# Counting the first 64 neighbours: triangular matmuls on TensorE against running sums along rows on VectorE

## The chip, the cores and the metric

The kernel runs on one core of a Trainium2 chip. The metric is the device time of one execution in microseconds (us). Five engines of the core work beside each other, each through its own queue in order: TensorE (PE in the profile), VectorE (DVE), ScalarE (ACT), GpSimd (POOL) and SyncE (SP, which here only issues transfers). They wait for each other by semaphores.

## The reference, cut to what matters

Four graph layers work on the same x (2708 x 512) and the same adjacency matrix adj (2708 x 2708, integers). Each layer's result is added to its input and normalised. The change concerns layer 0 and how its masks reach layer 1:

```python
# layer 0
Ab = A > 0
keep = Ab & (jnp.cumsum(Ab.astype(jnp.int32), axis=1) <= 64)      # the first 64 neighbours of each row
cnt = keep.sum(axis=1, keepdims=True)
nb_mean = (keep @ X) / jnp.maximum(cnt, 1.0)
xj = leaky_relu(nb_mean @ W_nb.T + b_nb)
xi = leaky_relu(X @ W_line.T + b_line)
x = layernorm(X + xi + jnp.where(cnt > 0, xj, 0))
# layer 1
mask = adj > 0                                                     # all neighbours
agg = mask @ x / jnp.maximum(mask.sum(axis=1, keepdims=True), 1.0)
x = layernorm(x + relu(concat(x @ W_self + b_self, agg @ W_nb + b_nb) @ W_comb + b_comb))
```

Layers 2 and 3 are attention over the same mask, and a small network at the end.

## The kernel before, in words

The 2708 rows are cut into NT = 22 tiles of 128 (the last has 20). Layers 0 and 1 run in four stages, which this text calls L0a, L0b, L1a and L1b.

**L0a, one t per row tile (lines 283 to 304).** Each t computes two products of x with a weight: P0 = x W_nb' into the single buffer pm0, and P1 = x W_line' into the single buffer pm1 (`product`, line 229: four matmuls of fp32, 512 columns wide, each in two passes). ScalarE and VectorE split P0 into a high and a low half, yH and yL, that stay in SBUF (lines 223, 224; yL frees pm0). P1 gets its bias and leaky ReLU on VectorE (298, 190; the add frees pm1), the row tile of x is added on GpSimd (300), and the sum goes to r0_dram (301). Beside this the adjacency matrix is brought in: `load_mask` (242) loads 128 rows of adj as bf16 through GpSimd's queue, `count` (248) makes them 0 or 1 on VectorE and sums each row, four small operations keep the row's counts (250 to 253), and `turn` (262, 266) transposes the row tile on PE, 22 transposes, and copies it as fp8 into maskT, from where every later layer reads it. maskT has one plane per tile j of neighbours, and in it one column per row of adj.

**L0b, masked sums (lines 311 to 429).** The row tiles are taken in blocks: first tiles 20 and 21, then five blocks of four. For each block and each of the 22 planes j, `kept` makes the operand kT: two matmuls of the 0/1 plane with constant triangles (line 319 with `upper`, line 409 with `below`) keep a running count in PSUM, and one VectorE operation (321) compares it with 64 and multiplies by the mask. kT has two buffers. Then, per row tile of the block, two matmuls add kT times yH and kT times yL (416): eight for a block of four. At the block's end ScalarE scales the sums by the reciprocal count (426). What follows (`finish`, lines 329 to 338) is a generator: one step of it is taken at each j of the next block. It adds the bias, applies leaky ReLU, adds r0, normalises and stores x1. Two more generators, `weights1` (products of layer 1's weights, on PE) and `vectors` (sums of weights for the later layers, on VectorE), are taken in steps beside it.

**L1a (lines 432 to 444)** makes two products per row tile of x1, with the same buffers pm0 and pm1. **L1b (445 to 464)** multiplies the whole mask with them: ScalarE casts planes of maskT to fp32r (455), PE takes 968 matmuls (458).

**The order of the work.** The program's order and priorities give each engine a fixed queue when the kernel is built. In L0a, `pe` chains some PE instructions by hand in program order. `issue_after` puts operations behind a named instruction of the program. [...] an engine whose next instruction waits lets everything behind it wait.

Of the kernel before, what the change touches and what calls it, by code (L numbers as in the profile page):

```python
# [9 lines left out]
F32 = mybir.dt.float32  # L10
F32R = mybir.dt.float32r
BF16 = mybir.dt.bfloat16
F8 = mybir.dt.float8e4
AF = mybir.ActivationFunctionType
OP = mybir.AluOpType
# [3 lines left out]
P = 128  # L19
D = 512  # L20
KD = D // P
EPS = 1e-5
ALPHA = 0.2
KEEP = 64.0
# [6 lines left out]
def kernel(  # L31
# [9 lines left out]
    nc = tc.nc  # L41
# [8 lines left out]
    def rows(t):  # L50
        return min(P, N - t * P)
# [24 lines left out]
    for c, value in ((iso, 0.0), (has, 0.0), (rdeg, 1.0), (rkeep, 1.0)):  # L76
        nc.vector.memset(c, value)
# [4 lines left out]

    maskT = big.tile([P, NT, NT * P], F8, name="maskT")
    nc.gpsimd.memset(maskT[:, NT - 1, :], 0.0)
    nc.gpsimd.memset(maskT[:, :, N:], 0.0)
# [47 lines left out]
    def transpose_weight(pool, psum, dst, src):  # L133

        for ki in range(KD):
            wr = pool.tile([P, D], F32, name="wr", bufs=4)
            nc.sync.dma_start(wr, src[ki * P:(ki + 1) * P, :])
            ps = psum.tile([P, KD, P], F32, name="ps_tr")
            for ko in range(KD):
                pe(nc.tensor.transpose(ps[:, ko, :], wr[:, ko * P:(ko + 1) * P], ident))  # L140
            nc.vector.tensor_copy(dst[:, :, ki * P:(ki + 1) * P], ps)  # L141
# [47 lines left out]
    def leaky(dst, u):  # L189
        nc.vector.scalar_tensor_tensor(dst, u, 0.01, u, op0=OP.mult, op1=OP.max)  # L190
# [7 lines left out]
    with ExitStack() as phase:  # L198
        yp = phase.enter_context(tc.tile_pool(name="y", bufs=1))

        upper = yp.tile([P, P], BF16, name="upper")
        make_upper_triangular(nc, upper)
        below = yp.tile([P, P], BF16, name="below")
        nc.vector.tensor_scalar(below, upper, -1.0, 1.0, op0=OP.mult, op1=OP.add)
# [16 lines left out]

        def keep_y(t, n, pm):
            nc.scalar.copy(yH[:n, t, :], pm[:n])  # L223
            return nc.vector.tensor_sub(yL[:n, t, :], pm[:n], yH[:n, t, :].bitcast(F32))
# [6 lines left out]

        def rows_of(src):
            return early(2, NT, lambda t: fetched(src, t, rows(t)))

        with ExitStack() as ph:
            st = ph.enter_context(tc.tile_pool(name="l0a", bufs=2))
            wnT, wlT = weight(), weight2

            def load_mask(t):
                n = rows(t)  # L240
                m = st.tile([P, N], BF16, name="m")
                nc.gpsimd.dma_start(m[:n], adj[t * P:t * P + n, :], max_dma_last_dim=N * 2)
                return m

            def count(t, m):
                n = rows(t)
                cnt = sm.tile([P, 1], F32, name="cnt")
                nc.vector.tensor_scalar(m[:n], m[:n], 0.0, None, op0=OP.is_gt, op1=OP.add, accum_out=cnt[:n])
                one = slice(t, t + 1)
                nc.vector.tensor_scalar(iso[:n, one], cnt[:n], 0.0, None, op0=OP.is_equal)  # L250
                nc.vector.tensor_scalar(has[:n, one], cnt[:n], 0.0, None, op0=OP.is_gt)
                nc.vector.tensor_scalar(rkeep[:n, one], cnt[:n], KEEP, 1.0, op0=OP.min, op1=OP.max)
                nc.vector.tensor_scalar(rdeg[:n, one], cnt[:n], 1.0, None, op0=OP.max)

            def turn(t, m, order=as_it_comes):
                n = rows(t)
                for g0 in range(0, NT, G):
                    g1 = min(g0 + G, NT)
                    ps = sums(BF16, (P, G, P))
                    for j in range(g0, g1):  # L260
                        w = rows(j)
                        order(nc.tensor.transpose(ps[:w, j - g0, :n], m[:n, j * P:j * P + w], identb[:n, :n]))
                    parts = [(P, g0, min(g1, FULL))] + ([(rows(FULL), FULL, NT)] if g1 > FULL else [])
                    for w, a, b in parts:
                        if a < b:
                            nc.scalar.copy(maskT[:w, a:b, t * P:t * P + n], ps[:w, a - g0:b - g0, :n],
                                           saturate=False)

            xs = rows_of(x)
            xTs = early(0, NT, lambda t, order=as_it_comes: transposed(ahead, ps_tr, xs(t), rows(t), "xT", order))
            ms = {}

            transpose_weight(st, ps_tr, wnT, l0_w_nb)
            lows = {}
            for t in range(2):
                xT = xTs(t, order=pe)
                lows[t] = keep_y(t, P, product(xT, P, wnT, 0, pe))
            transpose_weight(st, ps_tr, wlT, l0_w_line)  # L280
            b_line = bias(bcast(l0_b_line, D))
            for i in range(2):
                ms[i] = load_mask(i)
            for t in range(NT):
                n = rows(t)
                order = pe if t < 3 else as_it_comes
                if t > 1:
                    lows[t] = keep_y(t, n, product(xTs(t), n, wnT, 0, order))
                xT = xTs(t)
                if t + 1 < NT:  # L290
                    xTs(t + 1)
                for q in range(0 if t == 2 else t - 1, t) if t > 1 else ():
                    turn(q, ms[q], order)
                    if q + 2 < NT:
                        ms[q + 2] = load_mask(q + 2)
                pm = product(xT, n, wlT, 1, order)
                u = sm.tile([P, D], F32, name="u")
                nc.vector.tensor_add(u[:n], pm[:n], b_line[:n])
                leaky(u[:n], u[:n])
                nc.gpsimd.tensor_add(u[:n], u[:n], xs(t))  # L300
                nc.gpsimd.dma_start(r0_dram[t * P:t * P + n, :], u[:n])
                with tc.issue_after(lows[t].ins):
                    count(t, ms[t])
            turn(NT - 1, ms[NT - 1])
            nc.vector.reciprocal(rkeep, rkeep)
            nc.vector.reciprocal(rdeg, rdeg)

# [3 lines left out]
        with ExitStack() as ph:  # L311
            st = ph.enter_context(tc.tile_pool(name="l0b", bufs=1))
            b_nb = bias(bcast(l0_b_nb, D))
            cuts = [(b, min(b + 4, NT)) for b in range(0, NT, 4)]
            cuts = cuts[-1:] + cuts[:-1]

            def kept(cum, b, j):
                cols, w = slice(b[0] * P, b[1] * P), (b[1] - b[0]) * P
                nc.tensor.matmul(cum[:, :w], upper, maskT[:, j, cols], start=(j == 0), stop=True, skip_group_check=True)  # L319
                kT = st.tile([P, 512], F32R, name="kT", bufs=2)  # L320
                nc.vector.scalar_tensor_tensor(kT[:, :w], cum[:, :w], KEEP, maskT[:, j, cols],  # L321
                                               op0=OP.is_le, op1=OP.mult)
                return kT

            def begin(b):
                cum = ps_mm.tile([P, D], F32, name="pm0")
                return cum, kept(cum, b, 0)

            def finish(ts_, us):
                for t in ts_:  # L330
                    n, u = rows(t), us[t]
                    r0 = fetched(r0_dram, t, n)
                    nc.vector.tensor_add(u[:n], u[:n], b_nb[:n])
                    leaky(u[:n], u[:n])
                    yield
                    nc.vector.scalar_tensor_tensor(u[:n], u[:n], has[:n, t:t + 1], r0, op0=OP.mult, op1=OP.add)
                    layer_norm(sm, u[:n], n, u[:n])
                    nc.gpsimd.dma_start(x1_dram[t * P:t * P + n, :], u[:n])
                    yield
# [61 lines left out]
            todo, later = iter(()), chain(weights1(), vectors())  # L401
            cum, kT = begin(cuts[0])
            for i, b in enumerate(cuts):
                ts_ = range(*b)
                cols, w = slice(b[0] * P, b[1] * P), (b[1] - b[0]) * P
                pa = {t: sums() for t in ts_}
                for j in range(NT):
                    if j + 1 < NT:
                        nc.tensor.matmul(cum[:, :w], below, maskT[:, j, cols], start=False, stop=True,
                                         skip_group_check=True)  # L410
                        nxt = kept(cum, b, j + 1)
                    elif i + 1 < len(cuts):
                        cum, nxt = begin(cuts[i + 1])
# [5 lines left out]
                    next(todo, None)  # L419
                    if i == 1 and j > 1 or i > 1 and j % 2 or i == 0 and j == 2:  # L420
                        next(later, None)
# [6 lines left out]
            for _ in later:  # L428
                pass
# [4 lines left out]
            for t in range(NT):  # L434
                n = rows(t)
                xT = xTs(t)
                keep_y(t, n, product(xT, n, wnb[0], 0))
                if t + 1 < NT:
                    xTs(t + 1)
# [855 lines left out]
```

## Time and profile before

The three runs took 3095.4, 3096.92 and 3097.85 us. The profiled execution spans 3089.8 us at a mean granted clock of 0.99.

| Engine | busy, us | share of the span |
|---|---|---|
| PE | 2969.2 | 96% |
| VectorE | 1963.5 | 64% |
| ScalarE | 1411.1 | 46% |
| GpSimd | 239.6 | 8% |

| Stage | from, us | to, us |
|---|---|---|
| L0a | 0 | 214.9 |
| L0b | 214.9 | 532 |
| L1a | 532 | 694 |
| L1b | 694 | 921 |
| layers 2 and 3 | 921 | 3089.8 |

How to read it: the page gives busy time by engine, a table of 40 slices of about 77 us each, transfers, the chain that ended last, and groups of instructions. A group's row has the line, the engine, the operation, what it writes and reads with partitions x elements and type, a count, the busy time with the mean of one in ns, and the idle time of the engine just before with what ended it. In rows of waits, the numbers are the total in us, the times, and the longest. Durations of matmuls overlap, so their spacing is read from start times.

### The profile page before, as it was taken

The page shows a single profiled execution, that of the slowest core. Times are in us where ns is not written, and L with a number is a line of the kernel's source. Part 1 is how long each engine was busy: PE and PEld are TensorE (multiplying, and loading weights), DVE is VectorE, ACT ScalarE, POOL GpSimd, SP SyncE. Part 2 cuts the span into 40 slices and gives each one's busy share as a digit, 9 for nine tenths or more (in the row PEclk, how much of TensorE's full clock was granted, in tenths as well). Part 3 has the DMA queues.
Part 4 walks back from the last instruction along what each step waited for, and adds up shares of the span by engine and source line. Part 5 has one row for each costly group of instructions (what it writes and reads, how often), then busy time and mean ns, then how long its engine had stood idle before and what let it go on. Part 6 is the DMA issues. An engine that isn't in the chain of part 4 may idle for free. (4 is left out here: it accounts for less than half of the span.)

```text
span 3089.8 us, 36801 instructions
## 1 busy us (share of the span) xinstructions
PE 2969.2 (96%) x14714; PEld 1644.4 (53%) x14714; DVE 1963.5 (64%) x2495; ACT 1411.1 (46%) x1590; POOL 239.6 (8%) x378
## 2 busy tenths in 40 slices
PE   8999999999999999999998999999969999999997
PEld 4556666448888433444466333443446455555555
DVE  5662765212233899999976999999944535344242
ACT  2431000112225699999965899999942000001001
POOL 2220010101110000000012000000000000100001
PEclk9999999999999999999999999999989999999999
DMA  6651521312222001011034000000052000000000
GB/s 142 142 124 35 121 67 38 109 60 90 73 74 84 15 29 47 28 38 34 22 107 153 29 29 28 28 27 27 18 156 63 4 14 17 31 14 15 14 21 20
DMA packets 112920, 168.93 MB, mean 55 GB/s; under 512 B 39716, under 2 KB 63141, under 8 KB 112738
## 3 DMA queue, kind: packets, MB, share of 16 engines
q1 hardware_dynamic: 84066, 105.02, 11.4%
q0 software_dynamic: 18784, 57.79, 6.5%
q10 hardware_dynamic: 9888, 3.67, 0.5%
q8 instruction: 118, 1.93, 0.2%
q14 instruction: 64, 0.52, 0.1%
HBM read 136.46 MB, written 44.64 MB: 59 GB/s over the span
## 5 line engine op out<-in xcount | busy, mean ns | idle before, releaser
L624 DVE SCALAR_TENSOR_TENSOR e<-v_bc,ucol,maskT 128x1300 f32<-128x1300 f32 (+3 forms) x836 | 1183.2, 1474 | 335.0 <-PE pn L926 318.8
L632 ACT ACTIVATE c<-e,bcol 128x1300 fp8e4<-128x1300 f32 (+1 forms) x704 | 994.6, 1424 | 82.7 <-DVE e L624 32.8
L782 PE MATMUL po<-e,R 128*64 128x512 f32 (+2 forms) x4224 | 924.9, 549 | 29.9 <-DVE e L624 28.2
L782 PEld LDWEIGHTS po<-e,R 128*64 128x64 f32 x4224 | 349.0, 136 | 573.2 <-issue 383.2
L926 PE MATMUL pn<-e,R 128*128 128x512 f32 (+1 forms) x1056 | 415.1, 544 | 0.0
L926 PEld LDWEIGHTS pn<-e,R 128*128 128x128 f32 x1056 | 192.1, 191 | 199.8 <-issue 196.7
L416 PE MATMUL acc<-yH,kT 128*128 128x512 f32 x484 | 214.8, 444 | 0.0
L894 ACT ACTIVATE w<-pl,b 128x256 f32<-128x256 f32 (+1 forms) x88 | 40.9, 465 | 373.3 <-PE pl L892 373.3
L458 PE MATMUL acc<-yL,mf 128*128 128x512 f32 x484 | 192.9, 399 | 0.0
L416 PE MATMUL acc<-yL,kT 128*128 128x512 f32 x484 | 192.3, 397 | 0.0
L458 PE MATMUL acc<-yH,mf 128*128 128x512 f32 x484 | 190.5, 394 | 0.0
L117 POOL TENSOR_TENSOR ln_rs<-ln_rs,half 128x1 f32<-128x1 f32 x88 | 54.5, 620 | 1676.4 <-DVE ln_rs L116 1674.5
L561 PE MATMUL pm<-w,xT 128*128 128x264 f32 (+1 forms) x704 | 168.3, 394 | 10.7 <-DVE R L575 5.2
L229 PE MATMUL pm<-w,xT 128*128 128x512 f32 (+1 forms) x384 | 173.2, 593 | 2.4 <-ACT xT L130 1.4
L229 PE MATMUL pm<-weight,xT 128*128 128x512 f32 (+1 forms) x352 | 162.0, 604 | 3.6 <-DVE weight L141 2.8
L321 DVE SCALAR_TENSOR_TENSOR kT<-pm,maskT 128x512 fp32r<-128x512 f32 (+1 forms) x132 | 84.8, 642 | 123.5 <-PE pm L319 123.0
L892 PE MATMUL pl<-lin 128*128 128x256 f32 (+1 forms) x704 | 154.8, 374 | 2.8 <-DVE lin L811 2.8
L901 PE MATMUL pl<-lin,w 128*128 128x512 f32 (+1 forms) x352 | 157.4, 593 | 0.0
L561 PEld LDWEIGHTS pm<-w,xT 128*128 128x128 f32 (+1 forms) x704 | 129.6, 189 | 38.0 <-issue 5.8
L892 PEld LDWEIGHTS pl<-lin 128*128 128x128 f32 x704 | 130.6, 192 | 33.4 <-issue 15.8
L455 ACT CAST mf<-maskT 128x1024 fp32r<-128x1024 fp8e4 (+1 forms) x66 | 64.4, 977 | 163.4 <-PE acc L458 154.1
L223 ACT CAST yH<-pm 128x512 fp32r<-128x512 f32 (+1 forms) x44 | 25.7, 585 | 243.6 <-PE pm L229 243.6
(186 smaller groups left out, 2619.9 us busy)
## 6 DMA issues: line engine op xcount, KB each, us to landing
rows<-x_dram SPq DMA_DIRECT2D x63, 256.0 KB
m<-in_adj_dram POOLq DMA_DIRECT2D x21, 677.0 KB, 6.2
v_bc<-v_dram SPq DMA_DIRECT2D x16, 704.0 KB
x_dram<-u POOLq DMA_DIRECT2D x42, 256.0 KB, 2.3
v_bc<-v_dram SPq DMA_DIRECT2D x16, 650.0 KB
rows<-in_x_dram SPq DMA_DIRECT2D x21, 256.0 KB
r_dram<-u POOLq DMA_DIRECT2D x21, 256.0 KB, 3.2
rows<-r_dram SPq DMA_DIRECT2D x21, 256.0 KB
```

The source lines that it names most:

```text
L229: order(nc.tensor.matmul(pm[:n], xT[:, k, :n], w[:, k, :], start=(k == 0), stop=(k == KD - 1)))
L321: nc.vector.scalar_tensor_tensor(kT[:, :w], cum[:, :w], KEEP, maskT[:, j, cols], op0=OP.is_le, op1=OP.mult)
L416: nc.tensor.matmul(pa[t], kT[:, (t - b[0]) * P:(t - b[0] + 1) * P], y[:, j, :], start=(j == 0 and y is yH), stop=(j == NT - 1 and y is yL))
L455: nc.scalar.copy(mf[:, :g1 - g0, :], maskT[:, g0:g1, t * P:(t + 1) * P])
L458: nc.tensor.matmul(pa, mf[:, j - g0, :], y[:, j, :], start=(j == 0 and y is yH), stop=(j == NT - 1 and y is yL))
L561: nc.tensor.matmul(pm[a][:n, :D // 2 + heads], xT[:, k, :n], w[:, k, a, :D // 2 + heads], start=(k == 0), stop=(k == KD - 1))
L624: nc.vector.scalar_tensor_tensor(e[:, :w], v[:, :w], ucol[:, j, h:h + 1], maskT[:, j, c0:c0 + w], op0=OP.max, op1=OP.mult)
L632: nc.scalar.activation(c[:, :w], e[:, :w], AF.Sigmoid, bias=bcol[:, j, h:h + 1], scale=STEP, saturate=False)
L782: pe(nc.tensor.matmul(po[i][HO * k:HO * k + HO, :c1 - c0], R2[:, j, h * HO:(h + 1) * HO], e[:, c0:c1], start=(j == 0), stop=(j == NT - 1)))
L892: nc.tensor.matmul(pl[:, :w], self.lin1[:, k, f * P:(f + 1) * P], h[:, k, :w], start=(k == 0), stop=(k == KD - 1))
L901: nc.tensor.matmul(pl[:n], gT[:, f, (t - t0) * P:(t - t0) * P + n], self.lin2[:, f, :], start=(f == 0), stop=(f == KF - 1))
L926: nc.tensor.matmul(pn[k][:, :w], R2[:, j, k * P:(k + 1) * P], e[:, :w], start=(j == 0), stop=(j == NT - 1))
```

## The change

The counting on PE goes. Instead the count runs along the rows before they are turned:

- `count` moves to ScalarE: a sigmoid with a very steep slope makes the row 0 or 1 in place and sums it.
- `place` on VectorE: a scan adds along the row from -64.5 and takes the minimum with 0.5, in bf16; its product with the 0/1 row is negative for a kept neighbour, 0.5 for one that is dropped, 0 elsewhere. It is done in two parts of 1354 elements in L0a, and in four parts of 677 in L0b.
- `turn` copies to maskT with Sign: maskT now holds -1, 1 and 0.
- `kept` is one Relu of -maskT on ScalarE. No counting matmul and no VectorE operation is left in it.
- In L1a, one VectorE operation per plane (not_equal 0) makes maskT 0/1 again for all that follow.
- Fifteen of the 22 row tiles (HERE = 15, in the order of the blocks) are counted and turned in L0a, the first at t = 1 and with one t in six left out; the other seven go through a generator `other_masks`, ahead of `weights1` and `vectors`, one step at each j of L0b, in buffers lent by the weight tile "w" and by "spare". A turn in L0a comes at least a t after its count.
- All of L0a's PE instructions are chained by hand (`pe`).
- x is added in `finish`, from a second load, by VectorE; GpSimd's add goes. `finish` takes a step at every second j.
- The small operations on the counts are done per block (`reciprocals`) or once.
- The weights of layer 0 are staged in planes of maskT; the memsets of maskT come behind the first mask loads.

```diff
-            def count(t, m):
-                nc.vector.tensor_scalar(m[:n], m[:n], 0.0, None, op0=OP.is_gt, op1=OP.add, accum_out=cnt[:n])
...
+        def count(i, m):
+            nc.scalar.activation(m[:n], m[:n], AF.Sigmoid, bias=gate[:n], scale=STEP, accum_out=cnts[:n, t:t + 1])
+        def place(i, m, places, part, of):
...
+            nc.vector.tensor_tensor_scan(places[:n, :c1 - c0], m[:n, c0:c1], over[:n].to_broadcast([n, c1 - c0]),
+                                         places[:n, c0 - N * (part - 1) // of - 1:][:, :1] if part else -KEEP - 0.5,
+                                         OP.add, OP.min)
+            return nc.vector.tensor_mul(m[:n, c0:c1], m[:n, c0:c1], places[:n, :c1 - c0])
...
-                            nc.scalar.copy(maskT[:w, a:b, t * P:t * P + n], ps[:w, a - g0:b - g0, :n],
+                        nc.scalar.activation(maskT[:w, a:b, t * P:t * P + n], ps[:w, a - g0:b - g0, :n], AF.Sign,
...
+                now = counted < min(HERE, -(-t * HERE // (NT - 4)))
+                if now:
+                    m, places = masks(counted), st.tile([P, N // 2], BF16, name="places", bufs=1)
+                    with tc.issue_after(highs[t].ins):
+                        count(counted, m)
+                    with tc.issue_after(lows[t].ins):
+                        place(counted, m, places, 0, 2)
...
-                nc.gpsimd.tensor_add(u[:n], u[:n], xs(t))
...
+                if now:
+                    with tc.issue_after(low.ins):
+                        place(counted, m, places, 1, 2)
...
-            def kept(cum, b, j):
-                nc.tensor.matmul(cum[:, :w], upper, maskT[:, j, cols], start=(j == 0), stop=True, skip_group_check=True)
-                nc.vector.scalar_tensor_tensor(kT[:, :w], cum[:, :w], KEEP, maskT[:, j, cols],
-                                               op0=OP.is_le, op1=OP.mult)
...
+            def kept(b, j):
+                kT = st.tile([P, 4 * P], F32R, name="kT", bufs=2)
+                made = nc.scalar.activation(kT[:, :w], maskT[:, j, b[0] * P:b[0] * P + w], AF.Relu, scale=-1.0)
...
+                    nc.vector.tensor_add(u[:n], u[:n], x0)
...
-                        nc.tensor.matmul(cum[:, :w], below, maskT[:, j, cols], start=False, stop=True,
-                                         skip_group_check=True)
...
-                    next(todo, None)
-                    if i == 1 and j > 1 or i > 1 and j % 2 or i == 0 and j == 2:
-                        next(later, None)
+                    if j % 2:
+                        next(todo, None)
+                    with tc.issue_after(nxt_made.ins):
+                        next(both, None)
...
+                nc.vector.tensor_scalar(maskT[:, t, :], maskT[:, t, :], 0.0, None, op0=OP.not_equal, saturate=False)
```

## The prediction

> **What bounds the kernel now.** I read the slices of the page first: TensorE (PE) stands at 9 almost throughout. Then the busy times by stretch, cut where the stages of layers 0 and 1 begin and end by the times of their lines: L0a (projections, counting, turning of masks) 0 to 214.9 us, L0b (masked sums) to 532, L1a to 694, L1b to 921. The columns are PE, weight loads, VectorE (DVE), ScalarE (ACT), GpSimd (POOL), clock, DMA.
>
> ```profile
> 125.00:214.90 89.90, 89.90 (x443) 46.40 (x442) 54.39 (x99) 35.88 (x61) 24.77 (x29) 1.00 0.60 135
> 482.00:532.00 50.00, 49.56 (x214) 34.93 (x213) 25.50 (x48) 1.16 (x3) 5.14 (x8) 1.00 0.13 43
> 545.00:694.00 149.00, 149.00 (x406) 68.11 (x405) 34.73 (x56) 23.61 (x43) 14.47 (x27) 1.00 0.25 84
> 694.00:921.00 227.00, 227.00 (x975) 183.07 (x974) 64.41 (x128) 62.37 (x64) 24.54 (x44) 1.00 0.23 76
> ```
>
> PE has no idle time in any of them, so each microsecond taken from PE counts, and each wait given to PE counts. The groups by line show what the change removes (L319, L409: counting matmuls; L321, L248: DVE), and the waits show how little PE waits for:
>
> ```profile
> L321 DVE SCALAR_TENSOR_TENSOR kT<-pm,maskT 128x512 fp32r<-128x512 f32 (+1 forms) x132 | 84.8, 642 | 123.5 <-PE pm L319 123.0
> L248 DVE TENSOR_SCALAR_CACHE_REDUCE m<-m 128x2708 bf16<-128x2708 bf16 (+1 forms) x22 | 65.2, 2964 | 9.7 <-DMA m<-in_adj_dram 9.7
> L319 PE MATMUL pm<-maskT,upper 128*128 128x512 fp8e4 (+1 forms) x132 | 47.9, 363 | 0.0
> L409 PE MATMUL pm<-maskT,below 128*128 128x512 fp8e4 (+1 forms) x126 | 46.7, 371 | 3.6 <-DVE kT L321 3.6
> ```
>
> A matmul's duration overlaps its neighbours', so I price them by start times, in order of time on PE:
>
> ```profile
> 481.25 0.39 PE L409 MATMUL pm<-maskT,below 128*128 128x512 fp8e4 x1
> 481.48 0.38 PE L319 MATMUL pm<-maskT,upper 128*128 128x512 fp8e4 x1
> 481.50 0.59 PE L416 MATMUL acc<-yH,kT 128*128 128x512 f32 x1
> ...
> 483.80 0.38 PE L319 MATMUL pm<-maskT,upper 128*128 128x512 fp8e4 x1
> 483.82 0.59 PE L416 MATMUL acc<-yH,kT 128*128 128x512 f32 x1
> ```
>
> One j of a four-tile block takes 483.82 - 481.50 = 2.32 us. In L1b, where no counting runs, 968 matmuls (L458) take 225.8 us, 0.2333 each; eight are 1.87. So counting costs PE 0.45 us per j, and in the two-tile block (1.167 per j against 0.933) 0.23.
>
> [...]
>
> **The change, part by part.** DVE unit prices: from L248 (2708 elements, 2964 ns) and 512 elements at 690, one element costs 1.04 ns and an instruction 0.15 us.
> - Scan of 1354 elements: at half throughput 2 x 1354 x 1.04 + 150 = 2.96 us (bounds 1.56 at full rate, 4.4 at three cycles). Its product in bf16: 0.86 (1.56 at one per cycle). Quarters of 677: 1.57 and 0.51.
> - not_equal over 2816 fp8: 1.62 (bound 3.1).
> - Sigmoid over 2708 on ACT: 1.466 + 1300 x 0.833 ns = 2.55 us. Relu for kT: near 0.6 (the 512-wide copy L130, 585 ns).
>
> *L0b, PE.* Removed: 110 x 0.454 + 22 x 0.234 = **-55 us**. Seven turns arrive from L0a, 22 transposes in 1.42 us each (start times at 130.03 and 131.45): **+9.9**.
>
> *L0b, new waits.* kT moves from DVE to ACT, with two buffers: ACT may be late by at most one j. A Relu starts when j begins; a sigmoid behind it holds the next one. In the two-tile block (0.93 per j, Relu 0.4): 0.5 + 2.55 + 0.5 = 3.6 against two j = 1.9, so PE waits 1.7 us, and 2.2 at the second sigmoid, with a turn's last copies (0.72 and 0.26, the rows of L266) in the queue too; in the other blocks 0.6 + 2.55 + 0.6 = 3.75 against 3.73, with those copies 0.5 to 1.1 for each of five, 3.2 together. PE also waits in its queue at a turn until DVE has done the scans: a mask needs 4 x (1.57 + 0.51) = 8.3 us on DVE after its sigmoid. In the two-tile block PE gets there early: 14.4 us after L0b's begin for the second group of mask 15's transposes, which needs the last quarter, ready at 7.7 + 0.1 + 8.6 = 16.4; 2.0, and likewise 1.0 for mask 16. In the next blocks the built order lets six j (11 us) pass first; only for mask 20, whose scans stand behind 24 us of the previous block's finish (four tiles of nine DVE operations), do I find 3.6 us. Sum: 3.9 + 3.2 + 3.0 + 3.6 = **+14** (bounds 7 and 25). L0b: -55 + 9.9 + 14 = **-31**.
>
> *L0a.* Per t PE has 8.83 us (P0 to P0, 126.16 and 134.99), or 7.4 without a turn: seven turns gone, **-9.9**. On DVE the count (2.96 plus five small ones) goes; a t with a mask now has 3 x 0.69 + 2 x (2.96 + 0.86) = 9.7, about 9.4 since neighbours overlap by some 0.06. Fifteen masks fall on five of each six t. PE needs 5 x 8.83 + 7.4 = 51.6 us for six. DVE: the first mask's scan waits 2.5 for its sigmoid (put behind yH), 5 x 9.4, then P0 of the next t (3.6) waits until yL has freed the single pm0, then 1.5 to the next yL: 54.6. So DVE sets L0a: 3 x 3.0 = **+9**. L0a: **-1** (bounds -10 and +12). Mask loads (6.2 us to landing) land before ACT is ready for them. The added table load (1.28) and the scan ahead of the fourth weight copy lie in the start, where PE already waits 2.8 for that copy; some 1.8 is in the bounds.
>
> *L1a.* The 22 not_equal: in the built order eleven run in L0b's last block, under 41 us of PE, eleven at L1a's beginning. There DVE has, before the first yL, four of them (6.5) and nine finish operations (6.1): yL(0) comes some 16 us after L0b's end in place of 8, and the second product needs pm0. **+7.5**; the later ones add 1.2. Together **+9** (bounds 2 and 25).
>
> *At no cost.* POOL's add of x (27.9 us, L300) goes; its place, 22 DVE adds of 0.69 in finish, lies under L0b's PE, as do 22 more loads of x on SP's queue (DMA share 0.13 to 0.58). Weight rows stage in maskT: same transfers. The memsets of maskT (4.5 us) move behind the first mask loads, where POOL is idle for 24 us. POOL's later mask loads wait for turns, and the layer norm's pow stands behind them: DVE waits for pow, counted in the 3.6. L1b and all later layers read 0/1 masks as before.
>
> Sum against the profiled span: -31 - 1 + 9 = **-23 us**, 3089.8 to 3067. The other runs (3095.4 to 3097.9, median 3096.9) stand 7 us above the span, so I forecast 3074.
>
> **The rivals.**
> - *DVE hides everywhere.* For: DVE is busy only 54 of 90 and 25 of 50 us. Against: its queue is in order and carries the releases of pm0 and pm1. Then -55, and only the sigmoid waits (+7) stay: 3049.
> - *The bf16 product runs one per cycle.* [...] Then 15 x 1.4 = 21 us more in L0a, some 4 in L0b: 3074 + 25 = 3099, no change.
> - *Slower: the scan is dearer than half throughput.* At three cycles 1.4 more for each of 30 halves in L0a, 42 us, and 7 x 4 x 0.7 = 20 in L0b, of which some 15 reach PE: -23 + 57, 3131. It decides from about 0.55 us over 2.96 per half (23 / 42 of the step), 3.5 us. For: no scan is in the trace, and each has a scalar operand and a broadcast input. [...]
> - *PE doesn't get shorter* (the counting was hidden). L1b's 0.2333 per matmul, with the same weight loads, excludes it; I give it nothing.
>
> **How the numbers follow.** Likeliest 0.55, 3074, [...] (own range 3060 to 3086); hidden 0.18, 3049; product 0.13, 3099; scan 0.14, 3131. 3046 to 3098 leaves out the scan case, half of the product case and the fringe below. A measurement tells 0.2% (6 us) from no change: faster 0.55 + 0.18 + 0.01 = 0.74; within 0.11; slower 0.15.
>
> **What would show it.** Right: no L319 or L409; one j in blocks of four at 1.87 us; scans near 2.96 and 1.57 us, products 0.86 and 0.51, not_equal 1.62; L0a ending near 214, L0b taking some 286 us, L1a some 171; PE waits on ACT's kT of one or two microseconds after each sigmoid, and on DVE's yL in L0a and at L1a's start. Wrong: a scan above 3.5 us; PE waits at turns well beyond 10 us in all; L0a beyond 225; or no waits at all.

## The result, and the profile after

The changed kernel takes 3064.78 us (median of 3062.05, 3063.23, 3066.34 and 3068.42) against 3097.39 for the kernel before on the same chip: a ratio of 0.9896, 95% interval 0.9879 to 0.9914, or 32.6 us less. The prediction was 3074.

The busy times by stretch, cut where the four stages begin and end, of the kernel before and then of the changed one (columns: length, then PE, weight loads, DVE, ACT and POOL with their instructions, clock, DMA share, GB/s):

```profile
0.00:214.90 214.90, 202.12 (x957) 107.20 (x958) 124.51 (x216) 78.91 (x131) 60.90 (x76) 0.99 0.62 139
214.90:532.70 317.80, 314.20 (x1327) 215.22 (x1327) 176.89 (x319) 22.08 (x40) 24.69 (x38) 0.99 0.24 66
532.70:694.50 161.80, 161.08 (x440) 73.67 (x438) 42.50 (x71) 26.32 (x48) 16.14 (x30) 1.00 0.26 86
694.50:920.70 226.20, 226.20 (x971) 182.77 (x971) 64.11 (x127) 62.37 (x64) 24.33 (x43) 1.00 0.23 76
```

```profile
0.00:221.40 221.40, 197.63 (x802) 98.91 (x802) 160.78 (x151) 101.19 (x138) 30.01 (x48) 0.98 0.47 110
221.40:503.60 282.20, 270.05 (x1223) 204.06 (x1223) 174.61 (x274) 132.25 (x209) 32.10 (x41) 0.99 0.41 109
503.60:671.80 168.20, 163.12 (x441) 74.34 (x439) 68.58 (x91) 26.44 (x48) 21.55 (x32) 0.98 0.28 90
671.80:891.50 219.70, 219.70 (x971) 181.95 (x971) 64.13 (x127) 62.43 (x64) 24.34 (x43) 1.00 0.24 79
```

| Stage | before, us | after, us | difference | forecast |
|---|---|---|---|---|
| L0a | 214.9 | 221.4 | +6.5 | -1 |
| L0b | 317.8 | 282.2 | -35.6 | -31 |
| L1a | 161.8 | 168.2 | +6.4 | +9 |
| L1b | 226.2 | 219.7 | -6.5 | 0 |
| layers 2 and 3 | 2169.1 | 2173.1 | +4.0 | 0 |
| span | 3089.8 | 3064.6 | -25.2 | -23 |

The spans differ by 25.2 us and the medians by 32.6, because the profiled execution of the kernel before was short for its kind. A copy of that kernel with 32 bytes of padding (the second run below; its time is the same, ratio 1.0007) has a span of 3097.6, of which its layers 2 and 3 take 2174.8. Against that execution the stages differ by +5.8, -37.0, +6.4, -6.5 and -1.7: -33.0 us. So the +4.0 in the later layers is the difference between two executions and not a cost of the change.

The unit prices are in the groups by line and shape (busy time and mean ns of one, then idle time before):

```profile
L253 DVE TENSOR_TENSOR_SCAN places<-m,over 128x1354 bf16<-128x1354 bf16 x14 | 41.6, 2970 | 6.6 <-ACT m L247 6.3
L256 DVE TENSOR_TENSOR m<-m,places 128x1354 bf16<-128x1354 bf16 x28 | 24.1, 862 | 0.7
L253 DVE TENSOR_TENSOR_SCAN w<-w,over 128x677 bf16<-128x677 bf16 x16 | 25.7, 1609 | 24.2 <-ACT w L247 24.0
L484 DVE TENSOR_SCALAR maskT<-maskT 128x2816 fp8e4<-128x2816 fp8e4 x22 | 35.1, 1617 | 0.0
L247 ACT ACTIVATE m<-m,gate 128x2708 bf16<-128x2708 bf16 x14 | 35.7, 2553 | 0.0
L335 ACT ACTIVATE kT<-maskT 128x512 fp32r<-128x512 fp8e4 x110 | 68.8, 630 | 108.8 <-PE acc L459 108.8
```

Scan 2.97 us (3.03 for a row's second half), product 0.86, quarter scan 1.61, not_equal 1.62, sigmoid 2.55, Relu 0.63: all as priced, the quarter scan and the Relu 0.03 to 0.04 dearer.

Three of the prices on VectorE had no line behind them when they were forecast: the trace of the kernel before has no scan, no bf16 product and no not_equal on fp8. The changed kernel shows them. From a part of 677 elements to one of 1354 the scan adds 1.361 us (1609 to 2970 ns), so 2.01 ns per element, about twice the 1.04 ns that the forecast took from L248; the product adds 0.352 us (510 to 862 ns), so 0.52 ns per element, half of it; the not_equal, less 0.15 us for the instruction, comes to 0.52 ns for each of its 2816 elements. The sigmoid's price had lines in the trace before: 1466 ns for 1408 elements on ACT (L632), and 0.833 ns for each element more (L838: 1056 ns for 1024, 696 for 592).

What PE waits for, over layers 0 and 1 (the seven largest rows; total, times, longest):

```profile
PE pm L229 <- DVE yL L224: 9.3, 11, 1.6
PE ps_tr L137 <- POOL maskT L295: 6.2, 1, 6.2
PE pm L265 <- DVE spare L256: 6.0, 4, 2.4
PE pm L229 <- ACT xT L127: 5.8, 2, 5.1
PE pm L229 <- DVE weight L138: 5.2, 1, 5.2
PE acc L459 <- ACT kT L335: 4.3, 6, 1.6
PE pm L265 <- DVE w L256: 1.8, 1, 1.8
```

The 6.2 us are the start, before any weight is there (5.6 before). The rest is what the change made PE wait for: yL in L0a, the turns (6.0 and 1.8) and kT in L0b, and two single waits, of 5.2 us for a weight at the start and of 5.1 us for xT at L1a's begin. What the waits don't show is L1b: no PE wait there in either kernel, and still it takes 6.5 us less.

### The profile page after: what moved, and what is told of

It is laid out like the page before. It is cut to its first block, busy times and chain, and to the rows that moved or that the text cites. A ratio compares the mean times of both kernels' runs of the same rounds, so it can differ in the third digit from the quotient of the medians.

```text
span 3064.6 us, 36494 instructions
## 1 busy us (share of the span) xinstructions
PE 2918.2 (95%) x14456; PEld 1623.1 (53%) x14456; DVE 2021.9 (66%) x2408; ACT 1545.0 (50%) x1768; POOL 220.9 (7%) x354
## 5 line engine op out<-in xcount | busy, mean ns | idle before, releaser
L459 PE MATMUL acc<-yH,kT 128*128 128x512 f32 x484 | 197.3, 408 | 4.3 <-ACT kT L335 4.3
L459 PE MATMUL acc<-yL,kT 128*128 128x512 f32 x484 | 189.8, 392 | 0.0
L505 PE MATMUL acc<-yH,mf 128*128 128x512 f32 x484 | 188.4, 389 | 0.0
L505 PE MATMUL acc<-yL,mf 128*128 128x512 f32 x484 | 188.3, 389 | 0.0
L335 ACT ACTIVATE kT<-maskT 128x512 fp32r<-128x512 fp8e4 (+1 forms) x132 | 77.6, 594 | 118.8 <-PE acc L459 118.7
```

Source lines behind the costliest of these rows:

```text
L335: made = nc.scalar.activation(kT[:, :w], maskT[:, j, b[0] * P:b[0] * P + w], AF.Relu, scale=-1.0)
L459: nc.tensor.matmul(pa[t], kT[:, (t - b[0]) * P:(t - b[0] + 1) * P], y[:, j, :], start=(j == 0 and y is yH), stop=(j == NT - 1 and y is yL))
L505: nc.tensor.matmul(pa, mf[:, j - g0, :], y[:, j, :], start=(j == 0 and y is yH), stop=(j == NT - 1 and y is yL))
```

## The experiments

### Why do unchanged matmuls run faster?

In L1b both kernels run the same 968 matmuls on operands of the same types. The timeline of PE in the kernel before and in the changed one (start, duration):

```profile
799.64 0.39 PE L458 MATMUL acc<-yH,mf 128*128 128x512 f32 x1
799.87 0.40 PE L458 MATMUL acc<-yL,mf 128*128 128x512 f32 x1
800.10 0.39 PE L458 MATMUL acc<-yH,mf 128*128 128x512 f32 x1
800.33 0.40 PE L458 MATMUL acc<-yL,mf 128*128 128x512 f32 x1
```

```profile
690.04 0.39 PE L505 MATMUL acc<-yH,mf 128*128 128x512 f32 x1
690.27 0.39 PE L505 MATMUL acc<-yL,mf 128*128 128x512 f32 x1
690.49 0.39 PE L505 MATMUL acc<-yH,mf 128*128 128x512 f32 x1
690.72 0.39 PE L505 MATMUL acc<-yL,mf 128*128 128x512 f32 x1
```

The lines round to 10 ns. In the trace's nanoseconds, starts in the first are about 231 and 236 ns apart by turns, 0.2333 us on average; in the second they are 226 or 227 ns apart, in all but a handful of 967 gaps. The change removes the two triangles and adds a few small tiles, so every tile allocated after them has moved in SBUF. Four runs move tiles by padding alone (each pad and its memset):

```diff
+        pad1 = yp.tile([P, 8], F32, name="pad1")      # a1, a2, a3: ahead of yH
+        nc.vector.memset(pad1, 0.0)
         yH = yp.tile([P, NT, D], F32R, name="yH")
         yL = yp.tile([P, NT, D], F32R, name="yL")
+        pad2 = yp.tile([P, 8], F32, name="pad2")      # a3, a4: after yL
+        nc.vector.memset(pad2, 0.0)
```

The changed kernel with everything from yH on moved by 32 bytes (a1):

> The changed kernel with one more 32-byte tile per partition ahead of yH, so that yH, yL and every tile allocated after them (kT, mf) begin 32 bytes past a multiple of 64 instead of on one, as they did before the change. Theory A (the 32-row matmuls of layers 0b and 1b are spaced by where their operands lie): spacing of L459 and L505 back from 0.2267 to 0.2333 us, L0b about 288 us and L1b about 226 us, +13 us in all, about 3078. Theory B (the spacing fell because the counting matmuls are gone, or by the state of the clock): spacing stays at 0.2267, time 3065.

(By "32-row matmuls" the matmuls of L459 and L505 are meant; each has 128 rows.)

The kernel before with the same padding (a2):

> The kernel before with the same 32-byte tile ahead of yH, so that yH, yL, kT and mf now begin on a multiple of 64 bytes. Theory A: spacing of the two neighbour loops falls from 0.2333 to 0.2267 us, L1b from 226 to about 219.6 us, L0b from 317.6 to about 311, -13 us in all, about 3084. Theory B: no change, 3097.

The changed kernel with only y moved (a3), and with only what follows y moved (a4):

> The changed kernel with a 32-byte tile ahead of yH and another after yL: only yH and yL are off the multiple of 64 bytes, kT and mf are on one. If the moving operand y sets the spacing: 0.2333 us and about 3078, as with all shifted. If the loaded operand kT or mf sets it: 0.2267 us and 3065.

> The changed kernel with a 32-byte tile after yL only: yH and yL stay on a multiple of 64 bytes, kT and mf and the other tiles of later pools are 32 bytes off. If the loaded operand kT or mf sets the spacing: 0.2333 us and about 3078. If y sets it: 0.2267 us and 3065. If each has a part, about 3071 here and with y shifted.

Theory A fell: a1 kept 0.2267 us (3066.99 us, ratio 0.991, 0.9894 to 0.9927), a2 kept 0.2333 (3097.91, ratio 1.0007, 0.9998 to 1.0016). But a3 and a4 both went to 0.2333, with L1b at 226.1 us (3072.22 and 3072.49; ratios 0.9931, 0.9914 to 0.9948, and 0.9927, 0.991 to 0.9943). Neither operand's place decides, so perhaps the one relative to the other. The addresses in the built programs, kT (or mf, the same) minus y, over 256 bytes: 0 in the changed kernel and in a1; 32 in a3 and a4; 64 in the kernel before and in a2. Theory C says that this distance sets the spacing; two runs test it:

```diff
         yL = yp.tile([P, NT, D], F32R, name="yL")
+        pad1 = yp.tile([P, 48], F32, name="pad1")     # b1: the kernel before, 192 bytes; b2: the changed one, 16 (64 bytes)
+        nc.vector.memset(pad1, 0.0)
```

> The kernel before with a 192-byte tile after yL: y begins at 32 past a multiple of 256 bytes, and kT and mf now too (before: 96). Theory C (the spacing of these matmuls follows the distance of the loaded operand from y, taken over 256 bytes; it was 0 in the two kernels at 0.2267 us, 32 or 64 in the four at 0.2333): 0.2267 us on end in L1b, L1b about 219.7 us (226.2 before), L0b some 311 (317.6), about 3084. Theory D (the spacing is gained by what the changed kernel no longer does, or falls one way or the other in each execution): 0.2333, 3097, or a mixture.

> The changed kernel with a 64-byte tile after yL: kT and mf stand 64 bytes off y over 256, as in the kernel before. Theory C: spacing 0.2333 us with the pattern of the kernel before (236 and 231 ns by turns), L1b 226 us, about +13 us on the same start, 3072 to 3078. Theory D: 227 ns on end, 3065.

PE in L1b of b1 and then of b2:

```profile
800.03 0.39 PE L460 MATMUL acc<-yL,mf 128*128 128x512 f32 x1
800.25 0.39 PE L460 MATMUL acc<-yH,mf 128*128 128x512 f32 x1
800.48 0.39 PE L460 MATMUL acc<-yL,mf 128*128 128x512 f32 x1
800.71 0.39 PE L460 MATMUL acc<-yH,mf 128*128 128x512 f32 x1
```

```profile
799.82 0.40 PE L507 MATMUL acc<-yL,mf 128*128 128x512 f32 x1
800.05 0.39 PE L507 MATMUL acc<-yH,mf 128*128 128x512 f32 x1
800.28 0.40 PE L507 MATMUL acc<-yL,mf 128*128 128x512 f32 x1
800.52 0.39 PE L507 MATMUL acc<-yH,mf 128*128 128x512 f32 x1
```

Both answers came: the padded kernel before has the changed kernel's 227 ns, L1b 219.7 us, and takes 3088.34 us (ratio 0.998, 0.9971 to 0.9989, so 6 us less, 3 to 9 by the interval; half of the 13 expected). The padded changed kernel has the 231 and 236 ns of the kernel before, L1b 226.1, at 3068.85 us (ratio 0.9909, 0.9891 to 0.9928; the expected range began at 3072). Most of the missing half is L0b: it gained only 2.4 us in b1 and lost 1.0 in b2 (2.4 in a3, 4.7 in a4), where matmuls and other work alternate and 227 ns isn't held throughout: six in ten of L0b's starts are 226 to 228 ns apart in the changed kernel, three in ten in b1. So the address is worth 6.4 us in L1b and some 1 to 5 in L0b. By the stages that is 7 to 11 of the change's 33 us, by the time of b1 some 6, and it comes from where the tiles lie, not from the counting.

### What does VectorE's work in L0a cost?

```diff
-                    with tc.issue_after(lows[t].ins):
-                        place(counted, m, places, 0, 2)
...
-                    with tc.issue_after(low.ins):
-                        place(counted, m, places, 1, 2)
```

> The changed kernel without the scans and products of the 15 masks that are turned in L0a: the place of each neighbour within its row is left out there, so no neighbour of those rows is kept in layer 0. If VectorE sets the pace of L0a as the sum had it (three extra us per six blocks over the PE, 9 in all, and the scan ahead of the fourth weight copy 1.8): L0a 9 to 11 us shorter, about 211, time about 3055. If L0a is set by PE and the half clock at its start alone: within 3 us of the changed kernel.

3046.55 us (ratio 0.9849, 0.983 to 0.9867); L0a takes 201.0, 20.4 us less than in the changed kernel and twice what was expected. The stretches from the begin of the first P1 (32.7 and 24.9 us) on, of the changed kernel and then of this run:

```profile
33.00:221.40 188.40, 179.39 (x746) 88.62 (x745) 149.96 (x133) 93.73 (x130) 21.67 (x35) 0.99 0.44 100
```

```profile
25.00:201.00 176.00, 175.65 (x746) 89.04 (x746) 44.34 (x74) 94.44 (x132) 21.65 (x35) 1.00 0.46 107
```

With the same 746 matmuls and transposes, PE is idle for 9.0 us with scans and for 0.3 without: that is the bound by VectorE, 9 in the forecast. 3.7 us more are PE's own busy time. By start times 1.5 of them are the first P1, which takes 5.19 us there and 3.70 here (the next section says why), and the rest falls on the ten waits for yL, each of which costs some 0.2 us more than PE's idle time. The other 8 us lie ahead of this stretch: the first P1 begins at 24.9 us instead of 32.7. That is the start, and the next runs are about it.

### What delays the start?

P1 of the first block waits for the second weight. VectorE's timeline in the changed kernel:

```profile
26.11 1.28 DVE L138 COPY weight<-ps_tr 128x512 f32<-128x512 f32 x2
29.05 2.98 DVE L253 TENSOR_TENSOR_SCAN places<-m,over 128x1354 bf16<-128x1354 bf16 x1 [1.66 <-ACT m L247]
31.94 0.67 DVE L138 COPY weight<-ps_tr 128x512 f32<-128x512 f32 x1
```

The first scan stands ahead of the weight's fourth copy, and it first waits 1.66 us for the sigmoid on ACT. Also the first product P0 took 6.69 us in this execution, 3.70 in that of the kernel before. The clock goes with it: the first record of full clock is at 8.6 us in the kernel before, at 18.6 in the changed one, and at 10.2 in a3, whose L0a has the same instructions but for the padding; P0, which begins at 10.7, 12.6 and 12.0, takes 3.70, 6.69 and 3.70 us. Ahead of that the traces of the two kernels record no clock, but the matmuls show it: those of P0 start 0.85 us apart in the changed kernel up to 17.9 us and 0.43 in the kernel before, so this text calls it half clock there too. During PE's wait for the second weight the changed kernel has records of half clock (0.50), from 28.9 to 35.7 us, and the first part of P1 runs at it, with starts 0.85 us apart again:

```profile
32.66 5.19 PE L229 MATMUL pm<-weight,xT 128*128 128x512 f32 x8 [5.16 <-DVE weight L138]
```

Whether work on PE ahead of P0 brings the full clock sooner is shown by none of these traces. Two runs take the two causes apart, the clock alone (d1) and then both (f1):

```diff
+            warm = sums()
+            for _ in range(20):
+                pe(nc.tensor.matmul(warm[:, :P], ones, ones, start=True, stop=True))
             transpose_weight(room[:KD], ps_tr, wnT, l0_w_nb)
...
-                    with tc.issue_after(lows[t].ins):
+                    with tc.issue_after(low.ins if t == 1 else lows[t].ins):      # f1 only
                         place(counted, m, places, 0, 2)
```

> The changed kernel with 20 matmuls of ones ahead of the first transposes, between 1 and 6 us, when PE has nothing else; their result is not used. If the 4 to 8 us lost at the start are the half clock: full clock by about 12 us instead of 21 to 29, product of the first block 3.7 instead of 6.7 us, L0a end about 214 to 217 instead of 221, time about 3059. If the start is set by the weights' arrival: no change, 3065.

> The changed kernel with the warm-up matmuls of the run before and with the first scan issued on VectorE behind the fourth copy of the second weight instead of ahead of it. If that scan and its wait for the sigmoid (1.7 idle, 3.0 of scan) hold the weight and so the first product of the second weight: that product begins at about 26 us instead of 30.7 (warm) or 33.7 (changed kernel), L0a ends at 213 to 216, about 3060. If only the half clock counts: no better than the warm run, 3064.

The "21 to 29" of the first expectation are counted from the profile's zero, some 10.4 us ahead of the kernel's first instruction; from that instruction, as all other times here, they are 10 to 19. With the warm-up, PE had full clock from 6.9 us on (17.4 from the profile's zero), P0 took 3.70, and L0a ended at 219.1; but the time, 3064.32 (ratio 0.9899, 0.9883 to 0.9916), can't be told from the changed kernel's, so the 5 us expected of it were missed. Executions without a warm-up differ: P0 takes 3.70 us in a3, c1 and e1, and 5.1 to 6.7 in the changed kernel, a1, a4, b2 and g1. (In the three profiles of the kernel before, with and without padding, it is 3.70; whether the change makes a late start likelier stays open.) With the scan behind the copy, VectorE reads:

```profile
22.80 1.28 DVE L138 COPY weight<-ps_tr 128x512 f32<-128x512 f32 x2
24.23 0.69 DVE L138 COPY weight<-ps_tr 128x512 f32<-128x512 f32 x1 [0.15 <-PE ps_tr L137]
```

P1 begins at 25.0 us (29.6 with the warm-up alone, 32.7 in the changed kernel), L0a ends at 212.2, and the time is 3054.39 (ratio 0.9873, 0.9857 to 0.989). By the medians that is 10 us under the changed kernel, but the kernel before took 3092.82 beside this run and 3097.39 beside the changed kernel; by the ratios it is 7, against 5 expected, which the intervals don't exclude. P1's 4.7 us are the scan and its wait. The other 2.2 us of L0a are P1 itself, in the warm-up run and then in this one:

```profile
29.64 5.95 PE L229 MATMUL pm<-weight,xT 128*128 128x512 f32 x8 [5.16 <-DVE weight L138]
```

```profile
24.97 3.70 PE L229 MATMUL pm<-weight,xT 128*128 128x512 f32 x8 [0.78 <-DVE weight L138]
```

The warm-up run has half clock from 27.4 to 34.2 us, during P1's long wait and behind it; this one has none before 316.8.

### What does L1a pay for?

The forecast put +9 on the 22 not_equal. This run takes them out of L1a: the mask stays in signs through L1b, where ScalarE makes mf with Abs instead of a copy, and VectorE turns each column into 0/1 behind its block.

```diff
-                nc.vector.tensor_scalar(maskT[:, t, :], maskT[:, t, :], 0.0, None, op0=OP.not_equal, saturate=False)
...
-                    nc.scalar.copy(mf[:, :g1 - g0, :], maskT[:, g0:g1, t * P:(t + 1) * P])
+                    nc.scalar.activation(mf[:, :g1 - g0, :], maskT[:, g0:g1, t * P:(t + 1) * P], AF.Abs)
...
+                cols = maskT[:, :, t * P:(t + 1) * P]
+                nc.vector.tensor_scalar(cols, cols, 0.0, None, op0=OP.not_equal, saturate=False)
```

> The changed kernel with the 22 not_equal of L1a gone: L1b's ScalarE makes mf with Abs instead of a copy (the masks are still signs then), and after each of L1b's blocks VectorE turns the block's column of the mask into 0 and 1 for the later layers. If the not_equal on VectorE lengthen L1a, by 7 to 9 us as the sum had it: L1a 160 to 162 us instead of 168.6, L1b unchanged at 219.6, about 3057. If L1a's loss is its start (the wait for the first x1 and its turning, 5 us), it stays at 166 or more, 3062 to 3065.

3056.32 us (ratio 0.9881, 0.9865 to 0.9898; by the ratios 5 us under the changed kernel), L1a 161.9 as in the kernel before, L1b 219.7 with 36 us more work on VectorE, all hidden. So the not_equal are the cause. The way is not the forecast's, though. ACT and POOL at L1a's begin in the changed kernel, then ACT in a3:

```profile
504.85 1.36 POOL L384 DMA_DIRECT2D x_dram<-u  x1 [0.88 <-DVE u L116]
...
508.29 0.69 ACT L472 ACTIVATE u<-acc,rkeep 128x512 f32<-128x512 f32 x1 [4.22 <-DMA x_dram<-u]
508.88 1.06 ACT L127 COPY xT<-ps_tr 128x512 f32<-128x512 f32 x2
```

```profile
504.06 0.69 ACT L476 ACTIVATE u<-acc,rkeep 128x512 f32<-128x512 f32 x1 [0.25 <-DMA x_dram<-u]
504.65 1.06 ACT L127 COPY xT<-ps_tr 128x512 f32<-128x512 f32 x2
```

The last block's fourth u has one buffer. It is free when the previous block's fourth tile of x1 has been stored; that store comes at the end of nine VectorE operations of `finish`, which stand between not_equal of 1.6 us each. ACT waits 4.22 us for it, with L1a's first xT queued behind, and PE waits 5.1 for that xT:

```profile
509.51 5.70 PE L229 MATMUL pm<-w,xT 128*128 128x512 f32 x8 [5.08 <-ACT xT L127]
515.04 3.60 PE L229 MATMUL pm<-weight,xT 128*128 128x512 f32 x8
```

The clock is at half from 506.7 to 513.6, during the wait and behind it, so that the first product takes 5.70 us and the second 3.60; PE is busy 2.0 us longer in all (163.1 against 161.1 in e1). In a3 L0b ended at the same time, but VectorE reached the store 4 us earlier: it is in time, and L1a takes 162.9 with all its not_equal. Between these two runs it is a matter of who arrives first at L0b's end. The forecast's wait for yL exists too: g1, the next run, has it.

### What do the turns in L0b cost?

```diff
+                    for _ in range(4 if i < HERE + 2 else 1):
+                        yield
                     psum = (ps_mm.tile([P, G, P], BF16, name=f"pm{k % 2}") for k in range(3))
                     for _ in turn(i, m, lambda: next(psum)):
```

> The changed kernel with one step (j) more between the last product of a mask and its turning in L0b, four more for the two masks that fall into the two-tile block. If PE's waits for DVE ahead of the turns (7.8 us by the waits of the changed kernel) are net time: they go to under 2 us, L0b 276 to 278 instead of 282, about 3059. If the waits only move (to kT, or to the next weights): L0b stays within 2 us, 3063 to 3066.

PE's waits in L0b of this run:

```profile
PE acc L461 <- ACT kT L335: 4.2, 6, 1.6
PE ps_tr L125 <- DMA rows<-in_L_gnn_W_self_dram: 1.4, 1, 1.4
```

The 7.8 us of waiting for scans are gone; one wait of 1.4 us, for the rows of a weight, is new. L0b takes 273.3 us, 8.9 less, and the time is 3054.68 (ratio 0.9868, 0.9851 to 0.9884), 9 us under the changed kernel by the ratios. L1a is 2.3 us shorter as well, at 165.9, but still 4.0 longer than in e1. PE's waits in it:

```profile
PE pm L229 <- DVE yL L224: 3.5, 2, 2.3
PE pm L229 <- ACT xT L127: 0.8, 1, 0.8
```

Here VectorE has more work left at L0b's end, xT is in time, and PE waits for yL, as the forecast had it.

### The three together

> The changed kernel with the three edits of the runs before it together: warm-up and the first scan behind the second weight, turns of L0b's masks later, signs kept through L1a and L1b. If each removes a wait of its own, the savings add by stage: L0a 212 us, L0b 273, L1a 162, L1b 219.7, rest 2172, a span of 3039 and about 3040 (before 3094: ratio 0.9825). If two of them buy the same wait (the vectors' VectorE work, pushed to L0b's end, against L1a's start), L1a stays at 166 or L0b at 278: 3045 to 3050. If a later L0b or the column-wise not_equal beside L1b takes it back: 3055 or more.

3042.71 us (3040.12 to 3045.93), ratio 0.9827, 0.9813 to 0.984: 51 us under the kernel before and, by the ratios, 21 under the changed one. Its stages are 213.8, 273.9, 163.1, 219.8 and 2173.5 us: each saving stays, within 2 us.

## Why the prediction was right, and where it was not

**L0b, -31 (measured -35.6).** Right in mechanism and nearly in size. No counting matmul is left, and one j of a four-tile block takes 1.81 us against 1.87. The turn waits were 7.8 us against 6.6: in the two-tile block 1.75 and 1.03 against 2.0 and 1.0, ahead of mask 20 4.9 against 3.6. The kT waits were 4.3 against 7.1: the two in the two-tile block 3.2 together (1.7 and 2.2 forecast), the later ones 1.1 in all instead of 3.2. What was missing is the address: matmuls that the forecast took at 0.2333 us "with the same weight loads" ran at 0.2267 in part, 1 to 5 us.

**L0a, -1 (measured +6.5).** From the begin of the first P1 the sum held: 188.8 us before (from 26.1), 188.7 after (from 32.7); VectorE's bound is 9.0 us of idle PE, as computed (11 by start times), and the turns that left pay for it. What failed is the start, left to the bounds with "some 1.8". The scan ahead of the fourth copy was seen, but not that it waits for ACT's sigmoid: scan and wait hold P1 for 4.7 us (f1 against d1), where the kernel before had a count without the wait in that place. 3.0 us more are P0 at half clock in this execution (d1), which comes and goes. With neither, P1 begins 1.1 us earlier than in the kernel before (f1), so 6.6 are left.

**L1a, +9 (measured +6.4).** The cause was right (e1), the path wrong. The forecast had yL late, 16 us after L0b's end, and PE waiting for pm0; yL came after 12.5 and no PE wait on it is in L1a. PE waited for xT, behind ACT's wait for a store, which the forecast does not have. The wait for yL came to 3.5 us in g1 and to 0.5 in a3. So +9 is near 6.4 by another way than the one given; that part is luck.

**L1b, "as before" (measured -6.5).** The step that failed is the premise that equal instructions on equal types take equal time: the spacing of the 968 matmuls fell from 0.2333 to 0.2267 us, because the distance between their operands had changed (b1, b2).

**The sum and the rivals.** -23 against -25.2 between the profiled spans: the misses of +7.5 in L0a and -6.5 in L1b cancelled, by luck, so the sum is better than its terms. By the medians (-32.6), and against the longer profiled execution of a2 (-33.0), the change brought 10 us more than the sum. The address alone is about that much: without it some 22 to 27 us are left, an estimate from these runs. The time, 3064.78, is inside the forecast's range of 3060 to 3086 and 9 under its 3074. None of the rivals came: VectorE doesn't hide everywhere (c1, g1), the product takes 0.86 us and not the 1.56 of its rival, the scan 2.97 and not 4.4, and L0b did get shorter.

## What to carry to other kernels

When a queue in order takes on new work, look at what stands behind each new instruction at the seams of stages (a weight's last copy, the last store of a block) and at what that instruction itself waits for; here two seams and early turns cost some 21 us, and moving an instruction or a step took them back. When a change moves tiles, compare matmuls that it didn't touch before crediting the change; padding the old kernel tells the address from the idea.

## What the runs showed of the hardware that was not expected

The spacing of 128 x 512 fp32r matmuls with a new 128 x 128 weight each follows the distance of the loaded operand from the moving one in SBUF: 226 or 227 ns on end where it is a multiple of 256 bytes (the changed kernel, a1, b1 and all later runs, where the addresses are those of the changed kernel), 232 and 235 at 32 bytes over (a3, a4), 231 and 236 at 64 over (the kernel before, a2, b2), 3% in all. Moving both together changes nothing (0.2267 us in a1, 0.2333 in a2). Whether the period is 128 or 256 bytes, what a distance of 128 gives, and the mechanism were not tried, so they stay open.
